# An attention and mixture-of-experts kernel: who issues the transfers of the softmax denominators, who adds the merge, and when the reflections run

## The chip, the cores and the metric

The kernel runs on one core of a Trainium2 chip. A core has a matrix engine (TensorE, PE in the profile, with its weight loads listed as PEld), a vector engine (VectorE, DVE), a scalar engine (ScalarE, ACT), a general engine (GpSimd, POOL) and a queue engine (SyncE, SP), each working through its own list of instructions in order. Transfers (DMAs) are issued by an instruction on one of the queues, here SyncE's or GpSimd's, and land some time later. The metric is the device time of one execution in microseconds (us), smaller being better.

## The reference

Two layers follow each other on x (4 sequences of 512 tokens, 288 channels, float32). The first is a block with attention and experts, modulated by a condition c; the second rotates x in a subspace of 64 dimensions:

```python
mod = silu(c) @ w_adaln + b_adaln                 # six modulations
h = _modulate(_ln(x), sh_msa, sc_msa)
q, k, v = split(h @ w_qkv + b_qkv)                # 16 heads of 18
attn = softmax(einsum('bhqd,bhkd->bhqk', q, k) * hd ** -0.5)
o = (attn @ v).reshape(B, N, C) @ w_proj + b_proj
x = x + g_msa * o
xn = _modulate(_ln(x), sh_mlp, sc_mlp)
gates = softmax(top_k(xn @ w_gate, 2))            # 4 experts, 2 of them per token
x = x + g_mlp * sum_over_chosen(gate * (gelu(xn @ w1 + b1) @ w2 + b2))

U, _ = qr(P)                                      # P is 288 x 64
R = expm(A)                                       # A: skew, 64 x 64, from silu(cond) @ W.T + b
z = einsum('btn,nd->btd', x, U)
x = x + einsum('btd,nd->btn', z @ R - z, U)
```

## The kernel before

*Phases.* Up to about 27 us the modulations are computed. Then comes attention, to about 321 us, then the experts, to about 700 us, then the end (the rest of the rotation of the last tiles and the stores).

*Attention.* A sequence b has its 16 heads in four groups g, so there are 16 groups n = 4b + g (`NN` = 16), and each goes over four tiles of 128 keys (`NT` = 4), numbered t. This makes 64 steps (n, t). In each, `weigh` (L1772) makes the scores z by matmuls (L1780) and their exponentials es on ScalarE (L1789), and `gather` (L1793) of the step before adds up av by matmuls (L1798). PE's buffers for z come free when es has been taken.

*The denominators.* av of group n also holds the sum of the exponentials of each head. `normalize` (L1806) returns pieces that are called one after another, by `divide(n)`: the first copies av to oraw on ScalarE (L1815) and loads the four rows of sums into den, spread over 128 partitions, by four transfers (L1818); the next takes reciprocals on VectorE (L1824) and stores them to rdr in DRAM (L1826); the next reads them back, each row to the 32 partitions of its head, by four transfers (L1834, "spread"); the last multiplies (L1840, "divide"). All of these transfers are on SyncE's queue, which works in order: an issue that waits for its data holds up what is behind it.

*The merge.* When the four groups of a sequence are divided, `merge(b)` (L1852) multiplies by the projection for four token tiles (po, L1856), multiplies by the gate on VectorE (og, L1865) and adds that to x on GpSimd (L1866). `residual(b)` (L1844) has added the gated bias before, on GpSimd. `route(b)` (L1870) then takes the mean and variance (`statistics`, L1162: VectorE's BN instructions at L1167 and L1168, then on GpSimd the epsilon at L1169, the power -1/2 at L1170, and the negated product of mean and scale at L1174 and L1175), normalizes on ScalarE (xh, L1184), modulates and makes logits, top two, ranks and gates on VectorE (`choose`, L1903; one short step of it, the ratio, on ScalarE, L1963), and writes the tokens' rows to their experts' places by indirect transfers on GpSimd (L2119), each of which waits for the landing of the one before. They are called one or two at a time by `scatter_next`.

*The columns.* `column` (L1564) takes the next of 64 Householder reflections of the QR of P: some 22 instructions on VectorE, 5.4 to 5.7 us in all, depending on nothing but the column before. They are spread over the whole program as a filler for VectorE. Transposes and products of the rotation follow the last of them in the experts' phase (L1620, L1625).

*The order of the work.* It is written out by hand. The main loop (L2301 to L2364) keeps a dictionary `steps` from (group, tile) to a list of pieces, filled by `also`, and after `weigh` and `gather` of a step it calls that step's pieces in the order in which they were put there, then a piece of `beside` (other preparations), then one or two scatters. So where a piece stands in the list sets its place in each engine's order. In the list are: the pieces of `divide` for the group before; the merge of the sequence before in (1, 1) and (1, 2), two tiles each; `routing(b - 1)` from (1, 3) on, which puts its own pieces into later steps; `beginning(b + 1)` (statistics, normalization, transposes and values of the next sequence); `project` (queries and keys, L1727); and columns. The third sequence (b = B - 2) has its gates left for later (`late`).

*The passage to the experts.* `hidden(0)` begins right behind the last group's scores. The last groups' divides, the last merge and the remaining columns are pieces of the list `last_merge` (L2369), which go into `rest` (L2679); the loop over the experts (L2685 to L2711) calls one of them between its stretches of matmuls; None stands for a stretch without a piece. The loads of the experts' rows (xg, L2175 to L2180) and of their weights (w1s, w2s, L930) are on SyncE's queue, the first half's first rows on GpSimd's.

The functions that the change touches, and their callers:

Of the kernel before, what the change touches and what calls it, by code (L numbers as in the profile page):

```python
# [13 lines left out]
ALU = mybir.AluOpType  # L14
# [799 lines left out]
def fast_path(  # L814
# [142 lines left out]
    with ExitStack() as s1:  # L957
# [204 lines left out]
        def statistics(b, which):  # L1162
            st = small.tile([P, NT, 6], F32, tag="st", name=f"st{which}{b}")
            mv = small.tile([P, NT, 2], F32, tag="mv", name=f"mv{which}{b}")
            rs = small.tile([P, NT], F32, tag="rs", name=f"rs{which}{b}")
            for t in range(NT):
                nc.vector.bn_stats(st[:, t, :], xs[:, b * NT + t, :])  # L1167
                nc.vector.bn_aggr(mv[:, t, :], st[:, t, :])  # L1168
            nc.gpsimd.tensor_scalar_add(rs, mv[:, :, 1], LN_EPS)  # L1169
            nc.gpsimd.tensor_tensor(rs, rs, neghalf, ALU.pow)  # L1170
            if (b, which) != (0, 0):

                ms = small.tile([P, NT], F32, tag="ms", name=f"ms{which}{b}")
                nc.gpsimd.tensor_tensor(ms, mv[:, :, 0], rs, ALU.mult)  # L1174
                nc.gpsimd.tensor_scalar_mul(ms, ms, -1.0)  # L1175
                return ms, rs
            return mv, rs
# [628 lines left out]
        def normalize(n):  # L1806
# [4 lines left out]
            den = rt.tile([P, 2, N // HQ], F32, tag="den", name=f"den{n}", bufs=2)  # L1811
            rdr = dram.tile([4, N], F32, name=f"rdr{n}")

            def first():
                nc.scalar.copy(oraw, avs[n])  # L1815
                for h in range(4):
                    r = h * HQ + HD
                    nc.sync.dma_start(  # L1818
                        out=den[ts(h, HQ), 0, :],
                        in_=oraw[r : r + 1, :].rearrange("o (p c) -> o p c", c=N // HQ),  # L1820
                    )

            def reciprocals():
                nc.vector.reciprocal(den[:, 1, :], den[:, 0, :])  # L1824
                nc.vector.tensor_reduce(stat[:, :, n : n + 1], den, AX.X, ALU.add)
                nc.sync.dma_start(  # L1826
                    out=rdr.rearrange("h (p c) -> (h p) c", c=N // HQ), in_=den[:, 1, :]
                )

            def spread():  # L1830
                if g == 0:
                    oTs[b] = rt.tile([P, NG, N], F32, tag="oT", name=f"oT{b}")
                for h in range(4):
                    nc.sync.dma_start(  # L1834
# [7 lines left out]
            return first, reciprocals, spread, divide  # L1842
# [9 lines left out]
        def merge(b):  # L1852
            def tile_of(t):
# [12 lines left out]
                nc.gpsimd.tensor_tensor(xt, xt, og, ALU.add)  # L1866
# [402 lines left out]
        def routing(b):  # L2269
            def start():  # L2270
                norm, logits0, logits1, top, choices, ratio, gates_, *end = route(b)
                also((2, 1), norm)
                also((2, 2), logits0)
                also((2, 3), logits1)
                if b == B - 2:

                    also((3, 0), top, choices)
                    also((3, 3), ratio)
                    late.append(gates_)
                    return  # L2280
# [20 lines left out]
        for n in range(NN):  # L2301
            b, g = divmod(n, NG)
            if g == 0:
                steps = {(i, t): [] for i in range(NG) for t in range(NT)}
                for i in range(NG):
                    also((i, 0), lambda n=n + i - 2: divide(n))
                    for t in (2, 3):
                        also((i, t), lambda n=n + i - 1: divide(n))
                if b > 0:
                    merges = merge(b - 1)  # L2310
                    also((1, 1), *merges[:2])
                    also((1, 2), *merges[2:])
# [38 lines left out]
            for t in range(NT):  # L2351
# [4 lines left out]
                if len(held) > 1:  # L2356
                    gather_oldest()
                for piece in steps[g, t]:
                    piece()
                if beside:  # L2360
                    beside.pop(0)()
                scatter_next()
# [4 lines left out]
        for piece in beside:  # L2367
            piece()
        last_merge = [  # L2369
            lambda: (divide(NN - 2), divide(NN - 1)),  # L2370
            lambda: divide(NN - 1),
            column,
            lambda: divide(NN - 1),
            None,
# [7 lines left out]
    with ExitStack() as s2:  # L2382
# [296 lines left out]
        rest = [*last_merge, last_routing] + [column] * (len(chain) - 4)  # L2679
# [135 lines left out]
```

## Time and profile before

| | us |
|---|---|
| median of 4 executions | 721.27 (720.43 to 723.22) |
| profiled execution | 723.49 |
| its span | 721.8 |
| PE busy in the span | 673.1 |
| up to 26.6 us: PE busy | 19.93 |
| attention, 26.6 to 321.2: PE busy | 269.29 of 294.60 |
| experts, 321.2 to 700: PE busy | 371.29 of 378.80 |
| end, 700 to 721.8: PE busy | 12.62 of 21.80 |
| DVE, ACT, POOL busy in the span | 483.0, 289.9, 223.2 |
| mean granted TensorE clock | 0.977 of full speed |

The profile page gives busy times per engine and in 40 slices of the span (18 us each); an answer on waits gives, for each pair of instruction and releaser, how long the first engine stood idle for the second, how often, and the longest single time. A timeline lists instructions with start, duration and, in brackets, the idle time before with what ended it. A window's line gives the busy time of each engine and the clock granted to PE in that stretch: 0.50 is half of full speed. The time that PE stands idle is what can be won, and half clock makes the matmuls that follow longer.

### The profile page before, as it was taken

To read this page: it belongs to the slowest core of one execution; us is meant where nothing else is said; L and a number is where in the kernel's file an instruction comes from. 1 tells how busy PE (TensorE), PEld (TensorE's weight loads), DVE (VectorE), ACT (ScalarE), POOL (GpSimd) and SP (SyncE) were. 2 spreads that over 40 slices of the span, in tenths; PEclk is the share of its full clock that TensorE was granted. 3 is DMA by queue.
4 is the path that set the end of the run, shared out by engine and by line. 5 is a ranking of instruction groups with operands and counts; after the bars stand their busy time and mean duration, and the time that the engine had idled before them with its cause. 6 is when DMAs were issued, how large, how long until landed. Compare 5 with 4: busy or idle time off the path is not lost. (4 is left out here: it accounts for less than half of the span.)

```text
span 721.8 us, 11477 instructions
## 1 busy us (share of the span) xinstructions
PE 673.1 (93%) x3563; PEld 389.6 (54%) x3563; DVE 483.0 (67%) x2204; ACT 289.9 (40%) x465; POOL 223.2 (31%) x350
## 2 busy tenths in 40 slices
PE   6999698999989999597999999999999999999994
PEld 5422332434343434134577776777667777676763
DVE  5473858696877784783187788888888887004335
ACT  3566355475637554563134423222232232221232
POOL 3054922601242246630142163531303123031010
PEclk9999899999999999799899999999999999999999
DMA  9488812001100122336053352365324153205134
GB/s 214 135 240 207 281 46 53 21 17 46 49 20 17 45 86 84 106 87 161 9 168 75 102 168 83 124 164 165 84 83 142 23 171 80 82 25 190 42 119 168
DMA packets 70528, 75.47 MB, mean 105 GB/s; under 512 B 33452, under 2 KB 57746, under 8 KB 70458
## 3 DMA queue, kind: packets, MB, share of 16 engines
q1 hardware_dynamic: 60166, 47.78, 24.0%
q0 software_dynamic: 9792, 26.45, 12.2%
q10 hardware_dynamic: 500, 0.42, 0.3%
q8 instruction: 30, 0.49, 0.3%
q14 instruction: 40, 0.33, 0.1%
HBM read 52.13 MB, written 18.23 MB: 97 GB/s over the span
## 5 line engine op out<-in xcount | busy, mean ns | idle before, releaser
L2503 PE MATMUL pe<-w2s,hm 128*128 128x288 f32 (+1 forms) x648 | 163.7, 408 | 0.0
L2443 PE MATMUL ph<-xgT,w1s 128*128 128x288 f32 (+2 forms) x576 | 153.7, 417 | 0.4
L1789 ACT ACTIVATE es<-z 128x1024 f32<-128x1024 f32 x128 | 123.9, 1020 | 72.5 <-PE z L1780 71.1
L2503 PEld LDWEIGHTS pe<-w2s,hm 128*128 128x128 f32 (+1 forms) x648 | 118.7, 187 | 31.5 <-issue 2.3
L2443 PEld LDWEIGHTS ph<-xgT,w1s 128*128 128x128 f32 x576 | 107.1, 192 | 40.6 <-issue 11.6
L2465 ACT ACTIVATE hm<-ph,b1r 128x576 f32<-128x576 f32 (+2 forms) x72 | 49.9, 738 | 139.2 <-PE ph L2456 133.8
L1780 PE MATMUL z<-qk 32*128 32x512 f32 x512 | 91.4, 655 | 14.2 <-ACT es L1789 14.2
L1798 PE MATMUL av<-es,vt 128*32 128x512 f32 x512 | 70.8, 626 | 0.0
L2518 POOL TENSOR_TENSOR y<-y,gb 128x288 f32<-128x288 f32 x32 | 26.0, 812 | 126.3 <-ACT y L2517 126.3
L1780 PEld LDWEIGHTS z<-qk 32*128 32x128 f32 x512 | 27.1, 186 | 59.0 <-ACT es L1789 44.2
L2517 ACT ACTIVATE y<-pe,weight 128x288 f32<-128x288 f32 x32 | 16.0, 501 | 104.5 <-PE pe L2503 104.5
L1742 PE MATMUL pq<-hT,wqk 96*126 96x512 f32 (+3 forms) x120 | 56.6, 608 | 0.0
L2519 POOL DMA_INDIRECT chosen<-y,place x36 | 36.4, 1010 | 52.8 <-DVE y L2515 34.3
L1562 DVE SCALAR_TENSOR_TENSOR q<-q 64x1 f32<-64x1 f32 (+1 forms) x192 | 42.8, 223 | 6.9
L2119 POOL DMA_INDIRECT slots<-xr,where x32 | 32.7, 1023 | 47.3 <-DMA slots<-xr,where 38.4
L1856 PE MATMUL po<-wp,oT 128*128 128x288 f32 x128 | 35.1, 422 | 10.1 <-DVE oT L1840 10.1
L1754 POOL DMA_DIRECT2D qk<-row x42 | 21.5, 517 | 72.6 <-ACT row L1749 72.5
L1573 DVE STREAM_SHUFFLE wj<-pt 32x288 f32<-32x288 f32 (+47 forms) x96 | 42.1, 439 | 0.7
L1742 PEld LDWEIGHTS pq<-hT,wqk 96*126 96x126 f32 (+3 forms) x120 | 20.7, 183 | 33.8 <-issue 29.0
L1798 PEld LDWEIGHTS av<-es,vt 128*32 128x32 f32 x512 | 10.2, 109 | 49.7 <-issue 41.2
L1856 PEld LDWEIGHTS po<-wp,oT 128*128 128x128 f32 x128 | 23.8, 194 | 23.6 <-DVE oT L1840 11.5
L1840 DVE TENSOR_TENSOR oT<-oraw,oT 128x512 f32<-128x512 f32 x16 | 11.0, 688 | 36.8 <-DMA oT<-rdr 29.4
(281 smaller groups left out, 888.3 us busy)
## 6 DMA issues: line engine op xcount, KB each, us to landing
w2s<-in_w_dram SPq DMA_DIRECT2D x8, 1296.0 KB
w1s<-in_w_dram SPq DMA_DIRECT2D x8, 1152.0 KB
slots<-empty POOLq DMA_DIRECT2D x36, 148.0 KB, 3.3
oT<-rdr SPq DMA_DIRECT2D x64, 64.0 KB
qk<-row POOLq DMA_DIRECT2D x42, 72.0 KB, 2.6
yc<-chosen SPq DMA_DIRECT2D x4, 576.0 KB
out_dram<-xs SPq DMA_DIRECT2D x8, 288.0 KB
wr<-in_wrT_dram POOLq DMA_DIRECT2D x4, 567.0 KB
```

What stands on the lines that cost most here:

```text
L1562: nc.vector.scalar_tensor_tensor(s, u, part, s, ALU.mult, ALU.add)
L1573: nc.vector.stream_shuffle(wj[o : o + HQ, j:], pt[o0 : o0 + HQ, j:], [j % HQ] * HQ)
L1742: nc.tensor.matmul(pq[:n], wqk[:rows, k, item, :n], hT[:rows, k, :], start=(k == 0), stop=(k == NK - 1),)
L1780: nc.tensor.matmul(zs[c // 2][:, c % 2, :], qk[ts(c, HQ), 1, ts(t, P)], qk[ts(c, HQ), 0, :], start=True, stop=True,)
L1789: nc.scalar.activation(e, z, AF.Exp, scale=SCALE)
L1798: nc.tensor.matmul(avs[n][ts(c, HQ), :], vts[b % 2][:, t, 4 * g + c, :], es[c // 2][:, c % 2, :], start=(t == 0), stop=(t == NT - 1),)
L1856: nc.tensor.matmul(po, oTs[b][:, g, ts(t, P)], wp[:, g, :], start=(g == 0), stop=(g == NG - 1),)
L2119: nc.gpsimd.indirect_dma_start(out=slots[h], out_offset=bass.IndirectOffsetOnAxis(ap=where[:, i, t : t + 1], axis=0), in_=xrs[t // NT][:, ...
L2443: nc.tensor.matmul(ph[:, j, :SB], w1s[:, k, ts(f, P)], xgT[:, k, ts(j, SB)], start=(k == 0), stop=False,)
L2465: nc.scalar.activation(hm[:, f, : CAPS[r]].rearrange("p (j s) -> p j s", j=NB), ph[:, :, :SB], AF.Gelu_apprx_tanh, bias=b1r[:, h, r, f : f ...
L2503: nc.tensor.matmul(po[ts(m, rows), :], slots_[:, f, :], w[:, f, :], start=(f == 0), stop=(f == NF - 1),)
L2519: nc.gpsimd.indirect_dma_start(out=chosen[h], out_offset=bass.IndirectOffsetOnAxis(ap=place[:, t : t + 1], axis=0), in_=y, in_offset=None, ...
```

## The change

Five things are altered, in the order of the diff.

1. `statistics`: the epsilon is added on VectorE; the mean is negated on VectorE ahead of the power; GpSimd keeps the power and one product.
2. `normalize`: reciprocals and spread become one piece, `inverse`, so that the four loads of the spread are issued right behind the store of the reciprocals. For the last group (n = 15) the loads of den, the store to rdr and the spread are issued on GpSimd's queue, for the others on SyncE's as before. In the order of SyncE's queue only groups 2 and 3 differ: their spread now stands ahead of 6 and 17 small stores (udr, L1332).
3. `merge`: the sum with x is on VectorE. Two tiles of each merge now stand at the front of step (1, 2), ahead of the divide's piece there.
4. `routing` of the third sequence: the normalization and the logits come one step later each, the top two likewise; the ratio stays in (3, 3).
5. Columns of a step are called after its other pieces and the piece of `beside`. In `last_merge` a column comes first, the two pieces of groups 14 and 15 next, a stretch without a piece, the divide of group 15, and then a column; the list `rest` has one column fewer to place.

The order of TensorE's instructions is the same in both kernels.

```diff
--- before.py
+++ after.py
@@ -1166,13 +1166,14 @@
             for t in range(NT):
                 nc.vector.bn_stats(st[:, t, :], xs[:, b * NT + t, :])
                 nc.vector.bn_aggr(mv[:, t, :], st[:, t, :])
-            nc.gpsimd.tensor_scalar_add(rs, mv[:, :, 1], LN_EPS)
+            nc.vector.tensor_scalar_add(rs, mv[:, :, 1], LN_EPS)
+            if (b, which) != (0, 0):
+                ms = small.tile([P, NT], F32, tag="ms", name=f"ms{which}{b}")
+                nc.vector.tensor_scalar_mul(ms, mv[:, :, 0], -1.0)
             nc.gpsimd.tensor_tensor(rs, rs, neghalf, ALU.pow)
             if (b, which) != (0, 0):
 
-                ms = small.tile([P, NT], F32, tag="ms", name=f"ms{which}{b}")
-                nc.gpsimd.tensor_tensor(ms, mv[:, :, 0], rs, ALU.mult)
-                nc.gpsimd.tensor_scalar_mul(ms, ms, -1.0)
+                nc.gpsimd.tensor_tensor(ms, ms, rs, ALU.mult)
                 return ms, rs
             return mv, rs
 
@@ -1809,13 +1810,15 @@
             b, g = divmod(n, NG)
             oraw = rt.tile([P, N], F32, tag="oraw", name=f"oraw{n}", bufs=2)
             den = rt.tile([P, 2, N // HQ], F32, tag="den", name=f"den{n}", bufs=2)
+
+            queue = nc.gpsimd if n == NN - 1 else nc.sync
             rdr = dram.tile([4, N], F32, name=f"rdr{n}")
 
             def first():
                 nc.scalar.copy(oraw, avs[n])
                 for h in range(4):
                     r = h * HQ + HD
-                    nc.sync.dma_start(
+                    queue.dma_start(
                         out=den[ts(h, HQ), 0, :],
                         in_=oraw[r : r + 1, :].rearrange("o (p c) -> o p c", c=N // HQ),
                     )
@@ -1823,7 +1826,7 @@
             def reciprocals():
                 nc.vector.reciprocal(den[:, 1, :], den[:, 0, :])
                 nc.vector.tensor_reduce(stat[:, :, n : n + 1], den, AX.X, ALU.add)
-                nc.sync.dma_start(
+                queue.dma_start(
                     out=rdr.rearrange("h (p c) -> (h p) c", c=N // HQ), in_=den[:, 1, :]
                 )
 
@@ -1831,7 +1834,7 @@
                 if g == 0:
                     oTs[b] = rt.tile([P, NG, N], F32, tag="oT", name=f"oT{b}")
                 for h in range(4):
-                    nc.sync.dma_start(
+                    queue.dma_start(
                         out=oTs[b][ts(h, HQ), g, :], in_=rdr[h].partition_broadcast(HQ)
                     )
 
@@ -1839,7 +1842,11 @@
                 o = oTs[b][:, g, :]
                 nc.vector.tensor_mul(o, oraw, o)
 
-            return first, reciprocals, spread, divide
+            def inverse():
+                reciprocals()
+                spread()
+
+            return first, inverse, divide
 
         def residual(b):
 
@@ -1863,7 +1870,7 @@
                 xt = xs[:, b * NT + t, :]
                 og = small.tile([P, C], F32, tag="og", name=f"og{b}{t}", bufs=2)
                 nc.vector.tensor_mul(og, po, gates[:, 0, b, :])
-                nc.gpsimd.tensor_tensor(xt, xt, og, ALU.add)
+                nc.vector.tensor_add(xt, xt, og)
 
             return [lambda t=t: tile_of(t) for t in range(NT)]
 
@@ -2269,15 +2276,17 @@
         def routing(b):
             def start():
                 norm, logits0, logits1, top, choices, ratio, gates_, *end = route(b)
+                if b == B - 2:
+                    also((2, 2), norm)
+                    also((2, 3), logits0)
+                    also((3, 0), logits1)
+                    also((3, 1), top, choices)
+                    also((3, 3), ratio)
+                    late.append(gates_)
+                    return
                 also((2, 1), norm)
                 also((2, 2), logits0)
                 also((2, 3), logits1)
-                if b == B - 2:
-
-                    also((3, 0), top, choices)
-                    also((3, 3), ratio)
-                    late.append(gates_)
-                    return
                 also((3, 0), top, choices)
                 also((3, 1), ratio)
                 also((3, 2), gates_, *end[:1])
@@ -2304,12 +2313,12 @@
                 steps = {(i, t): [] for i in range(NG) for t in range(NT)}
                 for i in range(NG):
                     also((i, 0), lambda n=n + i - 2: divide(n))
-                    for t in (2, 3):
-                        also((i, t), lambda n=n + i - 1: divide(n))
+                    also((i, 2), lambda n=n + i - 1: divide(n))
                 if b > 0:
                     merges = merge(b - 1)
                     also((1, 1), *merges[:2])
-                    also((1, 2), *merges[2:])
+
+                    steps[1, 2][:0] = merges[2:]
                     also((1, 3), routing(b - 1))
                 else:
 
@@ -2355,10 +2364,15 @@
                 held.append((n, t, weigh(n, t)))
                 if len(held) > 1:
                     gather_oldest()
+
+                columns = [piece for piece in steps[g, t] if piece is column]
                 for piece in steps[g, t]:
-                    piece()
+                    if piece is not column:
+                        piece()
                 if beside:
                     beside.pop(0)()
+                for piece in columns:
+                    piece()
                 scatter_next()
                 if g in (0, 1, 3):
                     scatter_next()
@@ -2367,11 +2381,11 @@
         for piece in beside:
             piece()
         last_merge = [
+            column,
             lambda: (divide(NN - 2), divide(NN - 1)),
+            None,
             lambda: divide(NN - 1),
             column,
-            lambda: divide(NN - 1),
-            None,
             *merge(B - 1),
             *late,
         ]
@@ -2676,7 +2690,7 @@
 
 
         ROUTING = 13
-        rest = [*last_merge, last_routing] + [column] * (len(chain) - 4)
+        rest = [*last_merge, last_routing] + [column] * (len(chain) - 5)
         ends = basis + [None, all_fit, subspace, None] + [
             lambda n=n: early(n) for n in range(PAIRS + 1)
         ] + [None] * 4
```

## Prediction

> **What bounds the kernel now.** I read the page's busy times first, then its slices with the granted clock, then the list of waits, then the timelines of the engines around the two longest waits of TensorE.
>
> ```profile
> PE 673.1 (93%) x3563; PEld 389.6 (54%) x3563; DVE 483.0 (67%) x2204; ACT 289.9 (40%) x465; POOL 223.2 (31%) x350
> ...
> PE   6999698999989999597999999999999999999994
> ...
> PEclk9999899999999999799899999999999999999999
> ```
>
> TensorE is the bound: 673.1 of 721.8 us. No edit removes a matmul, so a gain can come only from the 48.7 us in which PE stands, and from the slices where the clock digit falls. The digits 5 and 7 on the PE row (17th and 19th slice) are the end of attention and the first expert; after them every digit is 9 until the last.
>
> ```profile
> ACT xh L1184 <- POOL ms L1175: 7.1, 1, 7.1
> ...
> PE z L1780 <- ACT es L1789: 14.2, 14, 8.1
> ...
> PE po L1856 <- DVE oT L1840: 10.1, 3, 5.8
> ...
> PE pt L1205 <- DVE brs L1323: 5.6, 1, 5.6
> ```
>
> Columns: total us, times, longest. The three longest single stops of PE are 8.1 (z behind es), 5.8 (the merge's po behind the divided oT) and 5.6 (pt behind brs, at 74 us). The first line explains the 8.1: ScalarE itself stood 7.1 us for one GpSimd result. Timelines of GpSimd, ScalarE and TensorE there (start, duration, then idle before and releaser):
>
> ```profile
> 293.63 0.99 POOL L2119 DMA_INDIRECT slots<-xr,where  x1 [0.39 <-DMA slots<-xr,where]
> 296.39 0.98 POOL L2119 DMA_INDIRECT slots<-xr,where  x1 [1.78 <-DMA slots<-xr,where]
> 297.45 0.23 POOL L1169 TENSOR_SCALAR rs<-mv 128x4 f32<-128x4 f32 x1
> 297.76 1.05 POOL L1170 TENSOR_TENSOR rs<-rs,neghalf 128x4 f32<-128x4 f32 x1
> 299.18 0.54 POOL L1175 TENSOR_SCALAR ms<-ms 128x4 f32<-128x4 f32 x1
> ```
>
> ```profile
> 299.75 2.18 ACT L1184 ACTIVATE xh<-xs,ms,rs 128x288 f32<-128x288 f32 x4 [7.09 <-POOL ms L1175]
> ```
>
> ```profile
> 302.90 2.13 PE L1780 MATMUL z<-qk 32*128 32x512 f32 x6 [8.06 <-ACT es L1789]
> ```
>
> GpSimd works in order: scatters, each behind the landing of the one before, then the statistics. The second hole, on SyncE's queue, VectorE and TensorE:
>
> ```profile
> 326.45 1.72 SPq L1834 DMA_DIRECT2D oT<-rdr  x4
> 328.27 2.41 SPq L1818 DMA_DIRECT2D den<-oraw  x4
> 331.57 0.41 SPq L930 DMA_DIRECT2D w2s<-in_w_dram  x1
> 332.11 0.76 SPq L1826 DMA_DIRECT2D rdr<-den  x1
> 333.54 6.09 SPq L2177 DMA_DIRECT2D xg<-slots  x4
> 340.30 1.86 SPq L1834 DMA_DIRECT2D oT<-rdr  x4
> ```
>
> ```profile
> 343.87 0.69 DVE L1840 TENSOR_TENSOR oT<-oraw,oT 128x512 f32<-128x512 f32 x1 [6.11 <-DMA oT<-rdr]
> ```
>
> ```profile
> 344.61 1.32 PE L1856 MATMUL po<-wp,oT 128*128 128x288 f32 x2 [5.77 <-DVE oT L1840]
> ```
>
> Group 15's denominators wait on SyncE's queue behind group 14's spread, its reciprocals' store behind w2s, its spread behind the xg loads. Both holes are followed by half clock:
>
> ```profile
> 343.50:350.30 6.80, 5.69 (x11) 3.83 (x12) 1.15 (x2) 0.00 (x0) 0.78 (x1) 0.50 0.01 2
> 299.10:309.35 10.25, 6.45 (x24) 1.73 (x24) 10.01 (x32) 5.94 (x8) 8.16 (x10) 0.50 0.77 224
> ```
>
> (Window, its length, busy times of PE, PEld, DVE, ACT, POOL, then the clock.)
>
> **The sum.** It is made against the profiled execution, 723.49 us (span 721.8 plus 1.7 around it), which stands 2.2 above the median of 721.27; 0.3% of that is 2.2 us, and less can't be told from no change.
>
> *Statistics and the merge's sum.* GpSimd loses two small operations per call (0.23 and 0.28 us) and the 16 sums (0.80 each, 12.6 in all). VectorE gains 15 small ones (0.19, the row of the 128x2 reduction: 2.9 us) and 16 sums of about 0.5 (the other 128x288 products, L1882 and L1883: 8 us). They fall before 293 us, where VectorE is busy 8.9 of 20 us from 280 to 300, or beside standing loads, so they cost nothing directly; were that cover gone, 11 us would lie on VectorE's chain, and about half of it on PE. VectorE no longer waits for GpSimd's sums (6.9 us in two waits), nor do the BN statistics (4.2).
>
> *First hole.* Scatters started at 283.90, 287.84, 290.67, 293.63, 296.39. Where no sum stands between two they are 2.8 apart, so without sums the last starts near 295.2 and ends at 296.2. The power (1.05) and one product (0.2) follow: 297.5 instead of 299.72, so 2.2 earlier. The norm also moves one step later, so on ScalarE the exponentials of (group 14, tile 2) go ahead of xh, and PE has one more step to do while ScalarE waits. xh runs from 297.5 to 299.7, and group 15's first z starts at about 300.7 instead of 307.68: 7.0 earlier. VectorE's chain is less lucky: logits follow xh, so they and all behind them (22.3 us without a pause, 300.46 to 322.78) gain only 2.1. The chain hands over once: ScalarE's ratio (319.99) then waits for the top-two at about 314.3, and the first expert's hidden layer starts near 315.8 instead of 321.20: 5.4 earlier. Late next is that chain.
>
> *Second hole.* Group 14's reciprocals come at about 321 (322.78 less 2.1). Its store and spread by SyncE take as long as now (323.04 to 328.17, then 1.8 to the divide): spread landed at 326.9. A column (5.5 us) now runs meanwhile. Group 15's raw copy is 5.4 earlier (ScalarE's, at 316), and its four denominator loads go by GpSimd, idle from 311.7 to 346.6 but for one 1.19 us gather; so they have landed long before, and reciprocals 15 follow divide 14 (0.69) at 327.7. The store is issued on GpSimd at about 328.2, past w2s and xg. Its latency isn't in the trace; GpSimd's nearest rows are 1.8 us (qk from last, 36 KB) and 3.5 (mdr, 4.5 KB); I take 3.3, near the row alike in size. Four spreads at 0.52 (qk from row, x42) are issued by 333.8 and land 1.8 (as SyncE's did) to 4.3 us later; I take 3.0, since w2s (1296 KB, 6.7 us on its own queue) and xg now run beside them. So divide 15 begins at 336.8 and ends at 337.5 instead of 344.56: 7.1 earlier, with bounds of 335.9 and 339.3. PE comes to that tile at 333.4 (338.84 less 5.4), and still stands about 4 us. Half clock: the 5.77 hole was followed by 6.8 us at half, the 8.06 one by 10.2, the 2.60 one (po at 124 us) by none. With one hole closed and the other at 4, I take off 1.5, with bounds of 0 and 2.8.
>
> *Order of reciprocals.* With the second half of the merge ahead of them, reciprocals 4, 8 and 12 come 4 to 7 us later (132.08 to about 136.5; 206.33 to 210.8; 278.70 to 285.4), since og waits for PE's po. Behind them stand the normalization of the next sequence on VectorE (+1.1 to +1.6 us) and PE's po at 199.16 (a hole of 1.73, +0.8; bounds 0 and 2). Group 2's spread passes the udr stores, so the hole at 124.04 (2.60) shrinks by 0.6 (bounds 0 and 0.9). The spreads placed behind the store wait 2.2 us on SyncE for the landing, and only udr stores stand behind them. Together +0.2, bounds -0.9 and +1.5.
>
> *Columns at the end of a step.* No column is added; one moves from before 410 us of the experts' part to ahead of the last divide, and VectorE's column chain, which feeds PE at 610.23 with 0.4 us to spare, gets shorter by 5.5. The wait at 74 us depends on group 0's spread (landed near 72) and one column and stays: 0 (bounds 0 and +0.5).
>
> Sum: 7.1 + 1.5 - 0.2 = 8.4 us less. 723.49 gives 715.1; the median gives 712.9, rounded to 713. The bounds (8.6 + 2.8 + 0.9 and 5.3 + 0 - 2.0) give 12.3 and 3.3 us less: 709.0 to 718.0.
>
> Two pages speak against this sum. The Trainium skill, "DMA: Bandwidth & Descriptors", section "Issuing engine by pattern", calls transfers from the sync and scalar queues generally faster than those from gpsimd; its table of first-byte latencies has 1 us against 0.6. For two transfers in series this would be an estimated 0.8 us of the gain; no run here shows it yet. "SBUF — State Buffer", section "SBUF: two separate sides", says that VectorE work holding the port it shares with GpSimd keeps GpSimd from writing descriptors. By it each of nine issues could wait for one VectorE operation of the column, 0.49 us in the trace, an estimate of 4.4 us less gain; the gather issued beside a column at 322.16 took 1.19 us against a mean of 1.06, which is far less.
>
> **The rivals.**
> *Half the gain* (chance 0.20): GpSimd's issues cost what its xg loads cost (0.88 instead of 0.52) and land as its slower rows (mdr 3.5 us, b2s 4.2): store from 328.2 to 332.6, spread issued by 336.1, landed at 340.3, divide ended at 341.0. That is 3.5 earlier with no relief of the clock: with the +0.2, 3.3 less, and down to 2.2 where the reciprocals' delay reaches PE: 718 to 719.1. For it: the other rows of that queue; against: those were issued beside heavy traffic.
> *The holes only move* (0.08): PE reaches the next wait earlier and stands there as long, as the 8.06 hole shrinks but VectorE's chain doesn't: within 2.2 us, 719.1 to 723.4. Against it: the second hole's end is set by SyncE's order, which does change.
> *Slower* (0.14): the last group's store and spread starve beside w2s and xg. There is such a row: group 0's store, issued at 55.85, was answered at 65.31, 9.5 us, beside the 4 x 567 KB of wr on the other queue. Then the store lands at 337.7, the spread is issued by 339.8 and lands after 5.7 (wg, GpSimd's row of 576 KB) at 345.5: divide ends at 346.2, 1.6 later; PE, from 333.4 on, stands 12.8 us and the half clock lengthens by 1.7 (half of 10.25 less 6.8); with +0.2 to +1.5 that is 3.5 to 4.8 more: 725 to 726. It decides from 14 us between the store's issue and divide 15; I work out 8.6. Against it: 1296 KB are no 2268.
>
> **How the numbers follow.** The forecast has the remaining 0.58, within 709 to 718. Below 709 I leave 0.05 of it (the second hole closed altogether). The range reaches over half the gain and most of the third case: 708.5 to 721.5, which leaves out about 0.05 below and 0.14 to 0.16 above. Faster: 0.58 + 0.20 less the little that reaches 719.1 = 0.77; same 0.08; slower 0.15.
>
> **What would show it.** The longest wait of xh for ms gone or under 5 us; group 15's first z near 300.7; hidden's start near 316; nine GpSimd transfers between 316 and 334; divide 15 near 337; po's longest wait near 4; no 10 us window at half clock at 300. Wrong would be: the spread landing after 342, a new hole of PE over 3 us between 130 and 290 us (the delayed reciprocals), or PE waiting at 610 us for the columns.

## The result and the profile after

The changed kernel takes 726.27 us (median; 723.16 to 731.9) beside 722.61 us for the kernel before. The ratio is 1.0047, 95% interval 1.0035 to 1.0058. It is slower by about 3.4 us by this ratio (3.7 by the medians); 713 had been forecast. Its profiled execution took 728.38 us, with a span of 726.7.

The page of the changed kernel, busy times and slices:

```profile
PE 680.6 (94%) x3563; PEld 393.2 (54%) x3563; DVE 490.2 (67%) x2235; ACT 290.3 (40%) x465; POOL 209.8 (29%) x328
...
PE   6998898999988997989899999999999999999995
...
PEclk9998999989999998999899999999999999999997
```

The 5 in the 17th slice is gone: the first hole has closed. There is a new 7 in the 16th, and TensorE is busy 7.5 us longer with the same matmuls; the mean granted clock is 0.969 instead of 0.977. The waits (total us, times, longest):

```profile
PE po L1863 <- DVE oT L1843: 13.6, 4, 4.7
...
PE z L1781 <- ACT es L1790: 7.9, 13, 2.8
```

The longest wait of z fell from 8.1 to 2.8 us, and ScalarE's wait of 7.1 us for ms is gone (the one that is left in the list, 1.3 us, is near 59 us). The merge's po now waits 13.6 us in four places instead of 10.1 in three. The largest of them, near 278 us, is where TensorE had no stop over 1 us before. VectorE's timeline, then TensorE's (start, duration, idle before and releaser):

```profile
253.65 0.69 DVE L1843 TENSOR_TENSOR oT<-oraw,oT 128x512 f32<-128x512 f32 x1
259.15 0.30 DVE L1488 COPY_PREDICATED XY<-need,psq 128x128 f32<-128x128 int32 x1 [4.81 <-PE psq L1438]
...
270.67 0.24 DVE L1827 RECIPROCAL den<-den 128x16 f32<-128x16 f32 x1
...
282.64 0.68 DVE L1843 TENSOR_TENSOR oT<-oraw,oT 128x512 f32<-128x512 f32 x1
```

```profile
283.38 2.29 PE L1863 MATMUL po<-wp,oT 128*128 128x288 f32 x4 [4.65 <-DVE oT L1843]
```

This is the place on which the result turns. The piece of `beside` in this step (group 12, tile 0) is a selection of XY by squares (psq) that TensorE has yet to compute. In the kernel before, the step's column came ahead of it, and VectorE worked on the column while it would have waited:

```profile
250.63 0.69 DVE L1840 TENSOR_TENSOR oT<-oraw,oT 128x512 f32<-128x512 f32 x1
...
256.73 0.28 DVE L1487 COPY_PREDICATED XY<-need,psq 128x128 f32<-128x128 int32 x1
...
262.64 0.24 DVE L1824 RECIPROCAL den<-den 128x16 f32<-128x16 f32 x1
...
274.37 0.67 DVE L1840 TENSOR_TENSOR oT<-oraw,oT 128x512 f32<-128x512 f32 x1
```

There the selection has no idle time in front. Now the column stands behind the selection; VectorE stands 4.81 us and then does the column. Reciprocals 11 come at 270.67 instead of 262.64, divide 11 at 282.64 instead of 274.37, and po, which needs group 11, stops. Of these 8 us, 3.0 were there already at divide 10 (253.65 against 250.63); the wait adds the other 5. The step (group 13, tile 1) takes 13.5 us instead of 6.1. The passage to the experts, on GpSimd, ScalarE and TensorE:

```profile
297.88 0.98 POOL L2126 DMA_INDIRECT slots<-xr,where  x1 [1.78 <-DMA slots<-xr,where]
298.94 1.04 POOL L1173 TENSOR_TENSOR rs<-rs,neghalf 128x4 f32<-128x4 f32 x1
300.07 0.20 POOL L1176 TENSOR_TENSOR ms<-ms,rs 128x4 f32<-128x4 f32 x1
```

```profile
305.29 2.17 ACT L1185 ACTIVATE xh<-xs,ms,rs 128x288 f32<-128x288 f32 x4
```

```profile
324.65 6.49 PE L2457 MATMUL ph<-xgT,w1s 128*128 128x320 f32 x16 [2.82 <-ACT xgT L2222]
```

TensorE came 10.4 us later to group 14's second half and therefore didn't have to wait for the power: the old hole was used up by a new one in front of it. The hidden layer starts 3.4 us later than before (321.20). ScalarE had four exponentials to do between ms and xh (305.29 instead of 299.75), but that isn't what delayed it: VectorE itself came late. Its timeline:

```profile
294.73 0.46 DVE L1872 TENSOR_TENSOR og<-po,gates 128x288 f32<-128x288 f32 x1 [0.92 <-PE po L1863]
...
295.66 0.25 DVE L1827 RECIPROCAL den<-den 128x16 f32<-128x16 f32 x1
...
301.60 0.69 DVE L1843 TENSOR_TENSOR oT<-oraw,oT 128x512 f32<-128x512 f32 x1 [2.73 <-DMA oT<-rdr]
...
308.64 1.10 DVE L1889 TENSOR_TENSOR xh<-xh,modrow 128x288 f32<-128x288 f32 x1
```

The merge waits for the late po until 294.73, the reciprocals of group 12 stand behind it, divide 12 waits for their spread, and a column follows. VectorE takes up xh at 308.64, without idle time in front, when ScalarE had long begun to deliver it. Then the last group, on GpSimd's queue, VectorE and TensorE:

```profile
337.36 0.59 POOL L1829 DMA_DIRECT2D rdr<-den  x1 [7.74 <-DVE stat L1828]
343.61 2.00 POOL L1837 DMA_DIRECT2D oT<-rdr  x4 [5.66 <-DMA rdr<-den]
```

```profile
347.44 0.69 DVE L1843 TENSOR_TENSOR oT<-oraw,oT 128x512 f32<-128x512 f32 x1 [10.15 <-DMA oT<-rdr]
```

```profile
348.18 1.33 PE L1863 MATMUL po<-wp,oT 128*128 128x288 f32 x2 [3.99 <-DVE oT L1843]
```

po's last tile resumes at 348.18 instead of 344.61. Each new stop is followed by half clock (0.50 in the column after the busy times):

```profile
281.70:288.52 6.82, 5.14 (x14) 3.24 (x14) 2.71 (x7) 0.00 (x0) 4.35 (x7) 0.50 0.26 82
346.55:353.37 6.82, 5.19 (x10) 3.53 (x11) 5.36 (x27) 0.00 (x0) 0.00 (x0) 0.50 0.02 5
```

### The profile page after: what moved, and what is told of

It is laid out like the page before. It is cut to its first block, busy times and chain, and to the rows that moved or that the text cites. A ratio compares the mean times of both kernels' runs of the same rounds, so it can differ in the third digit from the quotient of the medians.

```text
span 726.7 us, 11489 instructions
## 1 busy us (share of the span) xinstructions
PE 680.6 (94%) x3563; PEld 393.2 (54%) x3563; DVE 490.2 (67%) x2235; ACT 290.3 (40%) x465; POOL 209.8 (29%) x328
## 5 line engine op out<-in xcount | busy, mean ns | idle before, releaser
L2457 PE MATMUL ph<-xgT,w1s 128*128 128x288 f32 (+2 forms) x576 | 155.5, 421 | 3.2 <-ACT xgT L2222 2.8
L1863 PE MATMUL po<-wp,oT 128*128 128x288 f32 x128 | 39.4, 459 | 13.6 <-DVE oT L1843 13.6
L1863 PEld LDWEIGHTS po<-wp,oT 128*128 128x128 f32 x128 | 26.0, 212 | 28.6 <-DVE oT L1843 15.5
L1799 PEld LDWEIGHTS av<-es,vt 128*32 128x32 f32 x512 | 10.2, 109 | 50.0 <-issue 41.5
```

Of the source, the lines that this page charges most:

```text
L1799: nc.tensor.matmul(avs[n][ts(c, HQ), :], vts[b % 2][:, t, 4 * g + c, :], es[c // 2][:, c % 2, :], start=(t == 0), stop=(t == NT - 1),)
L1863: nc.tensor.matmul(po, oTs[b][:, g, ts(t, P)], wp[:, g, :], start=(g == 0), stop=(g == NG - 1),)
L2457: nc.tensor.matmul(ph[:, j, :SB], w1s[:, k, ts(f, P)], xgT[:, k, ts(j, SB)], start=(k == 0), stop=False,)
```

## The experiments

All times are medians; the ratio is to the kernel before, run beside them, with its 95% interval.

### The columns in their old place

```diff
-                columns = [piece for piece in steps[g, t] if piece is column]
                 for piece in steps[g, t]:
-                    if piece is not column:
-                        piece()
+                    piece()
                 if beside:
                     beside.pop(0)()
-                for piece in columns:
-                    piece()
```

> The changed kernel with one thing undone: columns are called at their place in the step's list again, ahead of the piece of beside. Theory A (a column behind the select of XY waits with it for PE's squares: VectorE stood 4.81 us at 254.34 for them, and reciprocals and divide of group 11 came 8.0 and 8.3 us later, so that the merge's po stopped 4.65 us at 278.73 and half clock followed): that stop falls under 1.5 us, the step of group 13, tile 1 takes about 6 us instead of 13.5, and the kernel gets 7 to 10 us faster than the changed one: 714 to 719. Rival B (the late reciprocals come from the merge's second half ahead of them and from the norm one step later): the stop stays above 3 us, and the time at 724 to 727.

Measured: 717.2 us, ratio 0.9907 (0.9878 to 0.9935). The selection of XY has no idle time in front, divide 11 comes at 276.33, po doesn't stop there, and the step of group 13, tile 1 takes 6.14 us. Theory A holds, and the one edit is worth 9 us: with it undone the rest of the change makes the kernel faster than before. What remains in this kernel, on ScalarE, TensorE and GpSimd:

```profile
323.60 0.20 ACT L1970 ACTIVATE g<-g 128x4 f32<-128x4 f32 x1 [6.11 <-DVE g L1966]
```

```profile
324.23 6.67 PE L2452 MATMUL ph<-xgT,w1s 128*128 128x320 f32 x16 [5.63 <-ACT xgT L2222]
```

```profile
331.50 0.59 POOL L1829 DMA_DIRECT2D rdr<-den  x1 [2.29 <-DVE stat L1828]
337.33 2.00 POOL L1837 DMA_DIRECT2D oT<-rdr  x4 [5.25 <-DMA rdr<-den]
```

The hidden layer starts as late as in the changed kernel, but the last group's store is issued 5.9 us earlier (331.50 against 337.36), divide 15 begins at 342.80, and TensorE doesn't stop at po. Of the 8.5 us between the two profiled spans, 5.1 lie there (the last po tile ends at 344.45 instead of 349.51). Of the other 3.4, 1.9 are half of the 3.86 us that were left of the half clock behind that stop (349.51 to 353.37), and about 1.7 come from 3.4 us of half clock near 713 us in the changed kernel, behind a stop of 2.00 us that this edit doesn't explain.

### Only the columns last

The kernel before with only that part of the change: the same lines, the other way round.

> The kernel before with one thing done: columns are called after the other pieces of the step and after the piece of beside; all else as before. Theory A: VectorE stands about 5 us near 254 for PE's squares, reciprocals 11 and divide 11 come about 8 us later, PE's po stops over 4 us near 275. GpSimd's long wait in front of group 15 is then partly met by a PE that comes later, so the time rises by 1 to 6 us: 723 to 728. Rival B (the place of the columns costs nothing, as I had forecast): the stop at po doesn't appear, and the time is within 2 us of the kernel before.

Measured: 726.95 us, ratio 1.0046 (1.0024 to 1.0067), as much as the whole change. On VectorE, then on TensorE:

```profile
258.64 0.30 DVE L1487 COPY_PREDICATED XY<-need,psq 128x128 f32<-128x128 int32 x1 [4.82 <-PE psq L1437]
```

```profile
282.85 2.77 PE L1856 MATMUL po<-wp,oT 128*128 128x288 f32 x5 [4.63 <-DVE oT L1840]
```

The same two waits, 4.82 and 4.63 us, with nothing else changed. The stop near 278 takes the place of the first hole (no stop of z is longer than 2.9 us now), and the hidden layer starts at 321.42 instead of 321.20. The loss comes out at the second hole: reciprocals 14 are 4.2 us later, divide 15 begins at 346.05 instead of 343.87, po stops 7.73 us instead of 5.77, and 10.2 us at half clock go with that stop instead of 6.8.

### Columns late, but ahead of `beside`

```diff
                 for piece in steps[g, t]:
                     if piece is not column:
                         piece()
+                for piece in columns:
+                    piece()
                 if beside:
                     beside.pop(0)()
-                for piece in columns:
-                    piece()
```

> The changed kernel with the columns called after the other pieces of their step, but ahead of the piece of beside. It parts two readings of the loss. Theory A1 (only the place behind beside costs: the select of XY makes VectorE wait for PE's squares, and the columns no longer cover that wait): VectorE's idle time of 4.81 us at 254 is gone, the po stop near 278 stays under 1.5 us, and the time is near that of the kernel with columns in their old place, 714 to 720. Rival A2 (columns late in a step cost wherever they are late, since the next step's reciprocals and divides come behind them): a po stop of over 3 us near 278, and 723 to 728. The hidden layer of the first expert should start near 319 instead of 324.2, since the top two no longer stand behind a column; but then PE should stop some 5 us at po near 337, so that it wins nothing at the end.

Measured: 719.49 us, ratio 0.9947 (0.9917 to 0.9976). No wait in front of the selection and no stop of po near 278: theory A1. It is the place behind the selection that costs, not that columns are last among their step's own pieces. As expected the hidden layer starts at 319.17, five us earlier than with the columns in place, and TensorE gives it back at po:

```profile
342.99 1.33 PE L1863 MATMUL po<-wp,oT 128*128 128x288 f32 x2 [5.96 <-DVE oT L1843]
```

### The norm a step earlier, with the columns late and in place

```diff
                 if b == B - 2:
-                    also((2, 2), norm)
-                    also((2, 3), logits0)
-                    also((3, 0), logits1)
-                    also((3, 1), top, choices)
+                    also((2, 1), norm)
+                    also((2, 2), logits0)
+                    also((2, 3), logits1)
+                    also((3, 0), top, choices)
```

> The changed kernel with the third sequence's norm, logits and top two a step earlier again. Theory A (the late hidden layer of the first expert follows VectorE's chain, and that starts with xh, which ScalarE took at 305.29 behind four exponentials though ms was there at 300.27): xh runs near 303.2, the logits start 2 us earlier, hidden(0) starts 2 us earlier than 324.65, and the time falls by about 2 us against the changed kernel: 723.5 to 725.5. Rival C (PE then stands for the exponentials that wait behind xh, and the time isn't better): group 15's first z starts 2 us later, and the time is 726 to 728.

Measured: 726.44 us, ratio 1.0039 (1.0015 to 1.0062): no gain, rival C in its time. xh ran at 303.05, 2.2 us earlier, but VectorE, still busy with what stands ahead, took it up only at 307.43. Group 15's first z came 1.3 us later (309.74), the hidden layer 0.7 us earlier (323.94), and po stopped 5.88 us instead of 3.99. An earlier xh wins little here, which confirms that VectorE's list and not xh was late.

> Columns in their old place, and the third sequence's norm and logits a step earlier again. Theory N (the norm a step later takes PE past the wait for the power, but the end of the chain is VectorE's, which starts with xh either way): PE's stop before a z near 297 grows from 3.1 to 6 to 8 us, hidden(0) starts within 1.5 us of 324.2, and the time is 716 to 719. Rival O (the norm a step later is what made the gain): hidden(0) starts 3 us or more later, and the time is 720 to 724.

Measured: 716.84 us, ratio 0.9912 (0.9882 to 0.9942). The time is that of theory N, its reason only in part: the stop before z grew from 3.08 to 5.17 us, but the hidden layer started 3.8 us earlier (320.45), which was not expected; po then stopped 2.04 us. Taken alone, the norm's place changes no time that can be told here. It moves the wait between three places.

### The last group by SyncE, with the columns late and in place

```diff
-            queue = nc.gpsimd if n == NN - 1 else nc.sync
+            queue = nc.sync
```

> The changed kernel with the last group's transfers on SyncE's queue, their order in the program the same. Theory D (GpSimd's queue wins little: its store took 6.25 us to land, 337.36 to 343.61, beside w2s and xg): divide 15 comes between 346 and 350 as against 347.44, and the time stays within 2 us of the changed kernel: 725 to 728. Rival E (the queue is the cause of the loss: SyncE's store would land in 3 us): divide 15 near 344, and 722.5 to 724.5. Rival F (GpSimd's queue is worth what I forecast): 729 or more, with denominators 15 landing after 337 and divide 15 after 350.

Measured: 730.37 us, ratio 1.0088 (1.0055 to 1.0122). Rival F: SyncE's store stands behind the xg loads. Its queue, then TensorE:

```profile
337.03 0.41 SPq L930 DMA_DIRECT2D w2s<-in_w_dram  x1
337.55 0.59 SPq L2182 DMA_DIRECT2D xg<-slots  x1
338.19 6.70 SPq L2184 DMA_DIRECT2D xg<-slots  x4
...
345.56 0.47 SPq L1829 DMA_DIRECT2D rdr<-den  x1
347.62 1.72 SPq L1837 DMA_DIRECT2D oT<-rdr  x4
```

```profile
351.76 1.33 PE L1863 MATMUL po<-wp,oT 128*128 128x288 f32 x2 [9.43 <-DVE oT L1843]
```

The store itself landed 2.1 us after its issue, against 6.25 on GpSimd's queue; but it was issued 8.2 us later, when the loads ahead of it had been issued.

> Columns in their old place, and the last group's transfers on SyncE's queue. With GpSimd's queue divide 15 began at 342.80 and PE didn't stop for it. Theory D1 (the queue is worth what it was worth with the late columns, where SyncE made 730.37 of 726.27): divide 15 near 345, a po stop of 2 to 4 us, and 719 to 722. Rival E1 (the queue was worth that only beside the late columns): divide 15 at or before 343, and 716 to 718.

Measured: 721.92 us, ratio 0.998 (0.9951 to 1.001). Theory D1 in its time: po stops 3.34 us and divide 15 begins at 343.31, though this execution was ahead (divide 11 at 273.78 against 276.33). Counted from divide 11, divide 15 comes 3.1 us later than with GpSimd's queue. The store, issued at 336.66 behind the xg loads, landed after 3.2 us.

### Only the queue

The kernel before, with only the nine transfers of the last group moved to GpSimd's queue (`queue` in place of `nc.sync` at L1818, L1826 and L1834).

> The kernel before with one thing done: the last group's nine transfers on GpSimd's queue. Theory D2 (as forecast, but with the store's measured 5.8 us in place of 3.3): denominators 15 land near 325.5, reciprocals 15 follow divide 14 at 330.7, the store lands near 337, divide 15 starts near 341.5 instead of 343.87, the po stop falls from 5.8 to about 3.5, time 718 to 721. Rival U (the transfers that leave SyncE's queue bring w2s and xg forward, and these delay the spread): divide 15 within 1 us of 343.87, time 720 to 724.

Measured: 718.16 us, ratio 0.9911 (0.9879 to 0.9944). One edit gives as much as all the parts together without the columns. Divide 15 begins at 339.10, earlier than the 341.5 expected, and po stops 1.29 us instead of 5.77. The first hole is as before, 8.04 us.

### The merge's sum on GpSimd again, columns in place

```diff
-                nc.vector.tensor_add(xt, xt, og)
+                nc.gpsimd.tensor_tensor(xt, xt, og, ALU.add)
```

> Columns in their old place, and the merge's sum on GpSimd again. Theory G (the sums interposed between the scatters hold up the statistics, as worked out: 2.2 us on GpSimd): the power of group 14's statistics starts 2 us later than 298.17, xh 2 us later than 299.58, hidden(0) 1.5 to 2.5 us later than 324.2, and the time is 718 to 721. Rival H (GpSimd's scatters wait for their own landings anyway and hide the sums): the power within 0.7 us of 298.2, and 716 to 718.

Measured: 719.8 us, ratio 0.9951 (0.9923 to 0.998). By absolute times this execution can't be set beside the other, as it was 5.0 us ahead at divide 11 (271.30). From there to the hidden layer it took 49.9 us instead of 47.9, and the stop before z was 4.97 us instead of 3.08: theory G, 2 us. The intervals of the two times overlap.

### The merge's second half behind the divide's piece

```diff
-                    steps[1, 2][:0] = merges[2:]
+                    also((1, 2), *merges[2:])
```

> The changed kernel with columns in their old place and the second half of each merge behind the divide's piece of its step again. Theory V (the delay of reciprocals 4, 8 and 12 costs little, as forecast, 0 to 2 us): reciprocals 12 come near 279 instead of 287.7, the stop of po at 199 falls under 1.8 us, and the time is 715 to 718. Rival W (the early merge is what brings the statistics of group 14 forward): the power is 2 us or more later than 298.2, and the time is 719 to 722.

With the columns in place, measured: 714.4 us, ratio 0.9875 (0.9849 to 0.9902), 2.8 us better than with the early merge and slightly under the range of theory V. From divide 11 to the hidden layer: 45.5 us instead of 47.9. The intervals of the two ratios overlap (0.9907 has 0.9878 to 0.9935). Two more kernels ask whether it holds elsewhere.

> The changed kernel with only the second half of each merge put behind the divide's piece of its step again; columns stay late. Theory X (the early merge is a second cause of the loss: reciprocals 12 stand behind it until 295.66, and VectorE then waits 2.73 us for their spread before divide 12, ahead of everything that leads to the hidden layer): reciprocals 12 near 289.6, that wait gone, hidden(0) 2 to 3 us earlier than 324.65, and 722.5 to 725. Rival Y (the late columns hide it): hidden(0) within 1 us of 324.65, and 725 to 728.

In the changed kernel itself: 724.41 us, ratio 1.0003 (0.9973 to 1.0033). Reciprocals 12 came at 291.89 and the wait in front of divide 12 was gone. From divide 11 to the hidden layer: 40.7 us instead of 42.0; po near 344 then stopped 5.60 us instead of 3.99. Theory X by its time, though the hidden layer gained 1.3 us and not 2 to 3: the early merge is a second, smaller cause, 1.9 us by the medians and 3.2 by the ratios, whose intervals lie just side by side (1.0033 and 1.0035).

> Columns in their old place, norm a step earlier, reciprocals 15 first in last_merge, two scatters behind the power, and now also the merge's second half behind the divide's piece. Theory X: the wait for the spread of group 12 goes, VectorE's chain and with it the ratio come 2 to 3 us earlier; what the xg loads then leave of it shows in the time, 709 to 713 against 713.4. Rival Z (in this kernel the xg loads, landed at 312.9, and not VectorE's chain set the hidden layer's start): the wait goes, hidden(0) starts within 1 us as before, and the time is 712.5 to 715.

In the last kernel of the next section: 710.81 us, ratio 0.9827 (0.9786 to 0.9867), beside 0.9865 (0.9834 to 0.9897) without it. The intervals overlap. From divide 11 to the hidden layer it was 43.7 us against 43.4, as rival Z has it; so what the early merge costs there isn't settled.

### Reciprocals 15 first, and the power ahead of two scatters

The first kernel has columns in place, the early norm, and this order:

```diff
         last_merge = [
-            column,
-            lambda: (divide(NN - 2), divide(NN - 1)),
+            lambda: (divide(NN - 1), divide(NN - 2)),
+            column,
             None,
```

> The changed kernel with columns in their old place, the third sequence's norm a step earlier again, and in last_merge the reciprocals of group 15 ahead of divide 14 and of the column (without that: store issued at 329.86, behind w2s at 326.76 and xg from 327.28, spread from 335.60, divide 15 at 339.38, po stop 2.04). Theory S (the store's 5.7 to 6.3 us are the time that w2s and xg take the transfer engines): reciprocals 15 near 325.5, the store issued ahead of w2s or with it and landed in 2 to 4 us, divide 15 at 331 to 335, no po stop over 1 us, time 713 to 716. Rival T (a store on GpSimd's queue takes 6 us in any case): issued near 326, landed near 332, divide 15 near 336; PE doesn't stop either, and the landing tells the two apart.

Measured: 715.17 us, ratio 0.9868 (0.9827 to 0.9909). po doesn't stop. GpSimd's queue, then SyncE's, then VectorE's timeline:

```profile
326.37 0.59 POOL L1829 DMA_DIRECT2D rdr<-den  x1 [0.43 <-DVE stat L1828]
329.56 2.00 POOL L1837 DMA_DIRECT2D oT<-rdr  x4 [2.61 <-DMA rdr<-den]
```

```profile
327.06 0.41 SPq L930 DMA_DIRECT2D w2s<-in_w_dram  x1
327.59 0.57 SPq L2182 DMA_DIRECT2D xg<-slots  x1
```

```profile
337.44 0.69 DVE L1843 TENSOR_TENSOR oT<-oraw,oT 128x512 f32<-128x512 f32 x1 [2.18 <-DMA oT<-rdr]
```

Issued 0.7 us ahead of w2s, the store landed within 3.2 us; issued 2.6 us behind it, in the kernel with the columns in place, 5.8. That is theory S for the store. The spread, now itself beside w2s and xg, landed 5.9 us after its last issue, and divide 15 began only at 337.44, later than the 331 to 335 expected. In the changed kernel, where the spread was issued behind the xg loads, it landed in 1.8 us. The traffic's toll moved from the store to the spread.

The second kernel also puts the two scatters of step (group 13, tile 2) behind the power:

```diff
-                scatter_next()
-                if g in (0, 1, 3):
-                    scatter_next()
+                if (n, t) != (NN - 3, 2):
+                    scatter_next()
+                    if g in (0, 1, 3):
+                        scatter_next()
+                if (n, t) == (NN - 3, 3):
+                    scatter_next()
+                    scatter_next()
```

> The same, and the two scatters of step (group 13, tile 2) are issued behind the power of group 14's statistics. Theory P (what is left of the stop of z near 297 is GpSimd's order: scatters 2.8 us apart ahead of the power, while VectorE had the statistics at 290.9): the power starts near 292.5 instead of 297.91, the stop of 5.17 us falls under 1.5 us, hidden(0) starts 1.5 to 4 us earlier, and the time is 710 to 714. Rival Q (VectorE's chain or the xg loads, which come behind the scatters, take over): the stop goes, hidden(0) starts within 1 us of the other's, and the time is within 1.5 us of the other's.

Measured: 713.39 us, ratio 0.9865 (0.9834 to 0.9897): the same ratio as the one before. The power starts at 292.02 and of the stop before z 0.84 us is left; but the xg loads, which come behind the scatters, now stop TensorE. Its timeline:

```profile
312.56 1.09 PE L2221 MATMUL pt<-ident,xg 128*128 128x128 f32 x4 [3.76 <-DMA xg<-slots]
```

The hidden layer starts at 319.59 instead of 321.45. Theory P for the mechanism, rival Q for the time. With the merge's second half put back this is the fastest kernel measured, 710.81 us; its interval lies below that of the kernel before and of the changed kernel, but overlaps with those of the two kernels of this section. In it the store stood behind w2s again, by 2.8 us, and took 6.5 us to land.

## Why the prediction was wrong

- *TensorE is the bound, and holes and half clock are what can be won.* Right. The kernels here differ in these two: the mean granted clock is 0.969 in the changed kernel, 0.977 in the one before and 0.987 in the fastest, with PE busy 680.6, 673.1 and 669.3 us.
- *Columns at the end of a step: "0 (bounds 0 and +0.5)".* This is the step that failed. It counted the columns that were moved and the chain at 610 us, but not what a column covered at its place: VectorE's wait for psq. With nothing else altered the move costs what the whole change costs (1.0046 against 1.0047); undone in the changed kernel, it gives 9 us, and the rest of the sum comes to 717.2 us, 4 short of the 713 forecast. The price is larger there, since VectorE, late from divide 11 on, still lags 5.9 us at the reciprocals of group 14 (4.2 in the other pair), so that divide 15 comes 4.6 us later (2.2), with half clock after it; why it lags more isn't shown. The sign named for being wrong, a new hole of over 3 us between 130 and 290 us, did come, but from the columns and not from the delayed reciprocals. Nor did the wait at 74 us stay: it fell from 5.6 to 2.7 us, and a stop near 61 us grew from 1.35 to 2.75. That VectorE's wait was 0 in the trace before was no evidence that it would stay 0.
- *First hole: 7.0 us earlier at group 15's first z.* The mechanism held where the columns were in place: 302.72, forecast 300.7. In the changed kernel the hole closed too, but there TensorE came 10.4 us later, and the late columns alone close it as well (1.07 us are left in the kernel with only them).
- *Hidden layer at 315.8.* Mis-sized, even with the columns in place: 324.23. The top two (expected at 314.3) stood behind a column from 315.79 to 321.34, after VectorE had waited 2.56 us for a spread; with the norm a step later they no longer come ahead of that column. In the kernel with the columns ahead of `beside`, where the column comes after them, it started at 319.17.
- *Second hole: divide 15 at 336.8.* The store's 3.3 us were 5.8 to 6.25; from its issue to divide 15 it took 10.1 us (changed kernel) and 11.3 (columns in place), not 8.6. No row gives the 6.7 us set there for w2s alone; in the trace before, w2s and xg together kept the DMA engines busy from about 332.5 to 341.5 us. The slower rival named 725 to 726 us, close to what was measured, but by luck: its limit of 14 us wasn't reached, and the time was lost elsewhere. The queue's worth was right in kind, and by the medians nearer to the 3.5 us of the second case: 4.1 us with the columns late, 4.7 with them in place, 4.4 alone (by the ratios 3.0, 5.3 and 6.4).
- *The rules weighed against it.* The Trainium skill, "DMA: Bandwidth & Descriptors", section "Issuing engine by pattern", calls the sync and scalar queues generally faster. The store's landing agrees on the face of it (2.1 and 3.2 us on SyncE's queue, 6.25 on GpSimd's), but not at the same moment: on GpSimd's queue it was 3.2 us too ahead of the big loads, so no run here parts the queue from the traffic. And GpSimd's queue won some 4 us, because what stood ahead in SyncE's order cost more. Of GpSimd's issues waiting for VectorE ("SBUF — State Buffer", section "SBUF: two separate sides") there was no sign: four loads of den were issued in 2.07 us beside a column's work at 326.13.
- *Order of reciprocals: +0.2.* Probably too small: by the medians 2.8 us with the columns in place and 1.9 in the changed kernel; in the last pair of kernels it isn't settled.
- *The norm a step later.* Counted as a help to TensorE. By itself it changes no time that can be told (717.2 against 716.84; 726.27 against 726.44).
- *The merge's sum.* Forecast 2.2 us on GpSimd in front of the power; 2.0 from divide 11 to the hidden layer.

## What to carry to other kernels

A filler that waits for nothing can be worth as much as the wait that it covers (here 4.8 us on VectorE, and 4 and 9 us in the end). Before moving it, look at which instruction follows it on its engine and when that one's input is ready; the trace before shows no wait there, because the filler hides it. And an edit that closes a hole should be priced together with the next wait on the same chain: here closing one hole often moved TensorE's stop to the next place, and so the norm a step earlier and the power ahead of two scatters won no time that can be told.

## What was not expected of the hardware

On GpSimd's queue a store of 8 KB took 3.2 and 3.7 us to land when it was issued just ahead of a load of 1296 KB on the other queue, and 5.6 to 6.5 us when it was issued behind that load (ten kernels). Stretches of half clock came in 3.4, 6.8 or 10.2 us, once 13.6, with stops of 1.3 to 8 us, but not with each: the stop of 1.35 us near 142 was followed by 6.8 us of half clock in the changed kernel and by none in the kernel before. Single executions of the changed kernel lie between 723.16 and 731.9 us, so that only medians over many, or times counted from a common event, could be compared.
